# Layer 0 attention from two score products instead of product features, with TensorE's instructions in program order

## The chip, the cores and the metric

The kernel runs on one core of a Trainium2 chip. The time is what the device takes for one execution, in microseconds (us). It is the median of 11 executions, and one more execution was taken with the hardware profiler on. Engines are named as in the profile: PE (TensorE, matmuls), PEld (its weight loads), DVE (VectorE), ACT (ScalarE), POOL (GpSimd) and SP (the queue that issues most of the transfers). L457 is line 457 of the kernel.

## What is computed

Two layers run over x of 32 sequences x 256 positions x 128 channels, in f32. Each layer normalizes x, computes attention `s` and a mixture of experts `g`, and adds `s * silu(g)` to x. Only the attention of layer 0 changes its arithmetic. Cut to what matters, for 16 heads of 8 channels:

```python
q1, k1, q2, k2 = rotary(x @ Wq1.T), rotary(x @ Wk1.T), rotary(x @ Wq2.T), rotary(x @ Wk2.T)
v = x @ Wv.T
s1 = einsum('bqhd,bkhd->bhqk', q1, k1)
s2 = einsum('bqhd,bkhd->bhqk', q2, k2)
pattern = where(causal, s1 / 8 * (s2 / 8), 0)
y = einsum('bhqk,bkhd->bqhd', pattern, v) @ Wout.T
```

There is no softmax: the pattern is a plain product of two scores. Layer 0's experts (8 experts, two per row, GELU, hidden size 512) and a shared expert read the same normalized x. Layer 1 has its own attention and experts.

## The kernel before

The 8192 rows lie in 64 tiles of 128 rows (partitions) by 128 channels. Four tiles make a panel of 512 rows (two sequences); there are 16 panels. Layer 0 runs in five parts:

1. **Start.** `begin` (L286) normalizes a panel, turns it with four transposes (`pst`), and computes the gate's `logit`. Behind each panel after the first, two steps of attention are emitted.
2. **Route and dispatch.** `route0` (L303) finds each row's two experts and slots. `dispatch` then scatters the 64 tiles twice by indirect DMA on POOL's queue (L158), 128 scatters. `pace` holds them three at a time: a small POOL memset, `breath` (L142), waits for the last three. Three of four scatters are followed by a step of attention.
3. **Experts.** `experts` (L572) runs 72 blocks of 256 rows: weights `wt` by an indirect DMA on POOL, rows `xd` by a load on SP's queue that waits for all scatters, two transposes (`xdt`), four up projections 256 wide (`eup`, L592), four GELUs on ACT (L597), eight down projections (`edn`, L604) of the block before, and an add on DVE (`od`). A step of attention follows every eighth of its four yields per block.
4. **Combine.** `combine0` gathers a panel's rows back (`rows`, L623: eight indirect DMAs per panel, 128 in all, also three at a time), weighs them on DVE (L632), applies SiLU on ACT (L641), multiplies on POOL (`soin`, L642), adds to x on DVE (L643), normalizes and computes layer 1's `logit`. A list of due times sets which of its six parts follows which step of attention, a panel every six steps.
5. Layer 1, which begins with its own attention at about 1256 us of the profile.

Attention is a generator, `attention0` (L514). It gives a step for each of eight head pairs of a sequence, 16 steps a panel, and interleaves the preparation of the next sequence (`prepare`, L377), the shared expert (`shared`, L479), the sums over values and the output projection (`outward`, L498).

Before the change, the product s1 * s2 is written as one inner product: the 64 products of the 8 channels of q1 and q2 make a feature vector, likewise k1 and k2. `prepare` projects (`psp`, L405), multiplies by cosines and sines on DVE (`tu`, L410), adds (`rot`, L418) and makes features (`feat`, L422: 1024 wide, on DVE, or on POOL beside the experts). `turn` (L440) transposes two heads' features at a time, four transposes, one ACT copy (L442). `pattern` then needs four matmuls over 64 rows (`pp`, L457) and one DVE instruction that multiplies by the causal mask (L459). Only the two diagonal blocks of 128 x 128 are computed so: the later half's queries see the first half through a `state` (`pss`, L429, masked on DVE at L432), and `values` adds the state's part (L469) and the diagonal blocks' part (L475) into `y`. So that four heads' values can be summed in place, `vz` holds each head's values in its own 8 of 32 columns, zero elsewhere.

PSUM has eight banks of 512 f32 columns: two for `turn`, two for `pp`, three for all other uses (`mm`), one for `y`. In layer 0 a scheduler sets the order of instructions on every engine, TensorE's too.

Lines that matter below, as they stand:

```python
nc.tensor.matmul(psp[:, w, c], lhsT=qk[r, 2 + c], rhs=qk[r, c], start=True, stop=True)   # L457
nc.vector.tensor_tensor(pat, psp, bc(bc(dmask, 1, 2), 1, 2), ALU.mult)                   # L459
nc.sync.dma_start(part[p], sos[p])                                                       # L511
nc.gpsimd.tensor_tensor(acc, acc, so[:, 0], ALU.mult)                                    # L642
```

Of the kernel before, what the change touches and what calls it, by code (L numbers as in the profile page):

```python
# [11 lines left out]
F32 = mybir.dt.float32  # L12
# [8 lines left out]
P = 128  # L21
# [35 lines left out]
def model_kernel(ctx: ExitStack, tc: tile.TileContext, a: dict, out: bass.AP):  # L57
# [163 lines left out]
    with ExitStack() as c0:  # L221
        w0 = c0.enter_context(tc.tile_pool(name="w0", bufs=1))
        wk = c0.enter_context(tc.tile_pool(name="wk0", bufs=2))
        ps_t = c0.enter_context(tc.tile_pool(name="ps_t", bufs=2, space=PSUM))
        ps_p = c0.enter_context(tc.tile_pool(name="ps_p", bufs=1, space=PSUM))
# [5 lines left out]
        cs = w0.tile([P, 2, 2, D], F32, name="cs")  # L231
# [6 lines left out]
        smask = w0.tile([P, NH // 2, 2, 32], F32, name="smask")  # L238
        dmask = w0.tile([P, P], F32, name="dmask")
# [15 lines left out]
        nc.scalar.dma_start(smask, a["smask"])  # L255
        nc.vector.tensor_scalar(dmask, tri, 1.0 / (D * D), None, ALU.mult)
# [28 lines left out]

        def begin(p, x):  # L286

            t = slice(p * TT, (p + 1) * TT)
            layernorm(wk, x, xn[:, t, :], TT)
            pst = mm_tile("pst")  # L290
# [4 lines left out]
            psg = mm_tile("psg")  # L295
# [4 lines left out]
            nc.vector.tensor_tensor(logit[:, t, :], pg, bc(gb, 1, TT), ALU.add)  # L300


        def route0():  # L303
            with ExitStack() as cr:
                rp = cr.enter_context(tc.tile_pool(name="rp0", bufs=1))
                (_, _, oh0), (_, _, oh1) = top2(rp, logit, NT)
                ohf, tot, pos = counted(rp, mm_tile, "g", oh0, oh1)

                psn = mm_tile("psn")
# [67 lines left out]
        def prepare(b, seq):  # L377
# [9 lines left out]
            xT = xTs[p]  # L387
            yield
            psv = mm_tile("psv")
            cols = [slice((b % 2) * S + c * P, (b % 2) * S + (c + 1) * P) for c in range(2)]  # L390
            for c in range(2):
                nc.tensor.matmul(psv[:, c * P : (c + 1) * P], lhsT=xT[:, cols[c]], rhs=wproj[:, 4, :],
                                 start=True, stop=True)
            v = wk.tile([P, P], F32, tag="v", name="v")
            nc.scalar.copy(v, psv[:, :P])
            pv = psv[:, : 2 * P].rearrange("p (i g j d) -> p i g j d", i=2, g=4, j=4)
            vz = vzs[b % 2]
            vv = vz.rearrange("p i (g j) (k d) -> p i g j k d", g=4, k=4)
            for j in range(4):
                nc.scalar.copy(vv[:, :, :, j, j, :], pv[:, :, :, j, :])  # L400
            seq.vz, seq.feat = vz, []
            yield
            for c in range(2):
# [5 lines left out]
                for u in range(2):  # L409
                    nc.vector.tensor_tensor(tu[:, u].rearrange("p (g d) -> p g d", d=D),  # L410
                                            psp.rearrange("p (g d) -> p g d", d=D),
                                            bc(cs[:, u, c, :], 1, 4 * NH), ALU.mult)
                yield
                r = wk.tile([P, 4, NH, D], F32, tag="rot", name="rot")
                rv = r.rearrange("p t h (u d) -> p (t h) u d", u=2)
                tv = tu.rearrange("p n (g u d) -> p n g u d", u=2, d=D // 2)
                for u in range(2):
                    nc.vector.tensor_tensor(rv[:, :, u, :], tv[:, 0, :, u, :], tv[:, 1, :, 1 - u, :],  # L418
                                            ALU.add)
                f = wk.tile([P, 2, NH * D * D], F32, tag="feat", name="feat", bufs=3)  # L420
                for n, eng in ((1, makers[1]), (0, makers[0])):
                    eng.tensor_tensor(f[:, n].rearrange("p (h i j) -> p h i j", i=D, j=D),  # L422
                                      bc(r[:, n], 3, D), bc(r[:, 2 + n], 2, D), ALU.mult)
                seq.feat.append(f)
                yield
            pss = mm_tile("pss").rearrange("p (m w c) -> p m w c", w=2, c=32)
            v4 = v.rearrange("p (w g c) -> p g w c", w=2, g=2)
            for m in range(NH // 2):
                nc.tensor.matmul(pss[:, m], lhsT=seq.feat[0][:, 1, m * P : (m + 1) * P],  # L429
                                 rhs=v4[:, m // 4], start=True, stop=True)  # L430
            seq.state = wk.tile([P, NH // 2, 2, 32], F32, tag="state", name="state")
            nc.vector.tensor_tensor(seq.state, pss, smask, ALU.mult)  # L432
            yield

        def turn(seq, m):

            pst = ps_t.tile([P, 512], F32, tag="t", name="ptr").rearrange("p (n c) -> p n c", n=4)
            for n in range(2):
                for c in range(2):
                    nc.tensor.transpose(pst[:, 2 * n + c], seq.feat[c][:, n, m * P : (m + 1) * P], ident)  # L440
            qk = wk.tile([P, 4, P], F32, tag="qk", name="qk", bufs=3)
            nc.scalar.copy(qk, pst)  # L442
            return qk


        pp = ps_p.tile([P, 2, 2, 2, P], F32, name="pp")
        turns = [0]

        def pattern(qk):

            pat = wk.tile([P, 2, 2, P], F32, tag="pat", name="pat", bufs=4)
            psp = pp[:, :, turns[0] % 2]
            turns[0] += 1
            for c in range(2):
                for w in range(2):
                    r = slice(64 * w, 64 * w + 64)
                    nc.tensor.matmul(psp[:, w, c], lhsT=qk[r, 2 + c], rhs=qk[r, c],  # L457
                                     start=True, stop=True)
            nc.vector.tensor_tensor(pat, psp, bc(bc(dmask, 1, 2), 1, 2), ALU.mult)  # L459
            return pat  # L460

        def values(y, seq, ms, done):

            first = ms[0] == 0
            last = ms[1] == NH // 2 - 1
            for w in range(2):
                for m in ms:
                    g = 2 * w + m // 4
                    nc.tensor.matmul(y[32 * g : 32 * g + 32, P:S], lhsT=seq.state[64 * w : 64 * w + 64, m, w],  # L469
                                     rhs=done[m][0][64 * w : 64 * w + 64, 1], start=first, stop=False)  # L470
            for c in range(2):
                for w in range(2):
                    for m in ms:
                        g = 2 * w + m // 4
                        nc.tensor.matmul(y[32 * g : 32 * g + 32, c * P : (c + 1) * P],  # L475
                                         lhsT=seq.vz[:, c, m + 8 * w, :], rhs=done[m][1][:, w, c],
                                         start=False, stop=last and c == 1)

        def shared(p, so):  # L479

            hs = wk.tile([P, NFC, PT], F32, tag="hs", name="hs")
# [6 lines left out]
            dn = mm_tile("dn").rearrange("p (i c) -> p i c", i=TT)  # L488
            for i in range(TT):
                for f in range(NFC):  # L490
                    nc.tensor.matmul(dn[:, i, :], lhsT=hs[:, f, i * P : (i + 1) * P],
                                     rhs=dnw[:, f, :], start=(f == 0), stop=(f == NFC - 1))
                if i < TT - 1:
                    yield
            nc.vector.scalar_tensor_tensor(so[:, 1], dn, 0.1, bc(dnb, 1, TT), ALU.mult, ALU.add)
            yield

        def outward(b, y):  # L498
# [11 lines left out]
            if b % 2:  # L510
                nc.sync.dma_start(part[p], sos[p])  # L511
            yield

        def attention0():  # L514


            order = (0, 4, 1, 5, 2, 6, 3, 7)
# [3 lines left out]
            ahead = turn(seqs[0], 0)  # L521
            owed = []
            tail = iter(())
            for b in range(B):
                seq = seqs[b]
                nxt = prepare(b + 1, seqs[b + 1]) if b + 1 < B else iter(())
                y = None
                done = {}
                for n, m in enumerate(order):
                    qk = ahead  # L530
                    if n < 7:
                        ahead = turn(seq, order[n + 1])
                    elif b + 1 < B:
                        for _ in nxt:
                            pass
                        ahead = turn(seqs[b + 1], 0)
                    done[m] = (qk, pattern(qk))
                    next(nxt, None)
                    if n % 2 == 0 and owed:
                        owed.pop()()  # L540
                    else:
                        next(tail, None)
                    if n % 2:
# [126 lines left out]
        def step():  # L670
# [6 lines left out]
            if n % 2:  # L677
                some(sh, 1)
# [519 lines left out]
```

## Time and profile before

| | us |
|---|---|
| median of 11 executions | 2210.42 |
| lowest, highest | 2204.13, 2217.14 |
| the profiled execution | 2209.47 |
| its span in the profile | 2207.7 |
| PE busy (share, instructions) | 1956.7 (89%, 18674) |
| DVE busy | 1234.3 (56%, 2609) |
| ACT busy | 968.4 (44%, 1977) |
| POOL busy | 659.1 (30%, 817) |
| mean granted clock of TensorE | 0.928 |

A group line of the profile names line, engine, operation, what it writes and reads, and a count; then busy time and mean nanoseconds of one, and the time its engine sat idle just ahead of it, with what ended that. Busy times of groups of one engine can overlap, since matmuls are pipelined. A wait line names who waited for whom, the sum, how often, and the longest. A shared column for "issue" is waiting that the profile can put down to nothing.

### The profile page before, as it was taken

The page shows a single profiled execution, that of the slowest core. Times are in us where ns is not written, and L with a number is a line of the kernel's source. Part 1 is how long each engine was busy: PE and PEld are TensorE (multiplying, and loading weights), DVE is VectorE, ACT ScalarE, POOL GpSimd, SP SyncE. Part 2 cuts the span into 40 slices and gives each one's busy share as a digit, 9 for nine tenths or more (in the row PEclk, how much of TensorE's full clock was granted, in tenths as well). Part 3 has the DMA queues.
Part 4 walks back from the last instruction along what each step waited for, and adds up shares of the span by engine and source line. Part 5 has one row for each costly group of instructions (what it writes and reads, how often), then busy time and mean ns, then how long its engine had stood idle before and what let it go on. Part 6 is the DMA issues. An engine that isn't in the chain of part 4 may idle for free.

```text
span 2207.7 us, 45584 instructions
## 1 busy us (share of the span) xinstructions
PE 1956.7 (89%) x18674; PEld 1441.7 (65%) x18674; DVE 1234.3 (56%) x2609; ACT 968.4 (44%) x1977; POOL 659.1 (30%) x817
## 2 busy tenths in 40 slices
PE   6999999699999998765969589999999995788898
PEld 4777677488888886544747466666677773556565
DVE  6666767432222224654768477777433335677776
ACT  5623333233334333434746346566311114565655
POOL 0005555413222222555530035544000004454300
PEclk9999999899999999877979789999999997788889
DMA  8702111135445443222220311110122212112100
GB/s 262 211 1 78 44 45 34 57 116 162 155 148 175 146 151 111 77 80 67 82 69 35 108 32 35 36 35 27 49 72 72 72 55 56 52 54 60 44 26 11
DMA packets 131456, 176.80 MB, mean 80 GB/s; under 512 B 16304, under 2 KB 94659, under 8 KB 131248
## 3 DMA queue, kind: packets, MB, share of 16 engines
q1 hardware_dynamic: 103056, 96.57, 13.6%
q0 software_dynamic: 26752, 76.03, 11.5%
q8 instruction: 148, 2.42, 0.5%
q10 hardware_dynamic: 1440, 1.27, 0.2%
q14 instruction: 60, 0.49, 0.1%
HBM read 104.78 MB, written 69.21 MB: 79 GB/s over the span
## 4 chain that ended last, share of the span: by engine, by line
PE 42%; DMA 4%; POOL 3%; ACT 3%; issue 2%; DVE 1%; POOLq 0%; ACTq 0%; DVEq 0%; SPq 0%
PE apsT L853 6%; PE apav L862 6%; PE mpsd L1027 5%; PE mpsu L1014 5%; PE apsc L838 3%; PE apsc L831 2%; DMA rows<-moe,gidx 2%; PE pp L457 2%; DMA rows<-moe,slot 1%; POOL rows L623 1%; PE apsf L873 1%; PE apsv L815 1%; POOL rows L1055 1%; PE ptr L440 1%; PE apsk L803 1%
## 5 line engine op out<-in xcount | busy, mean ns | idle before, releaser
L457 PE MATMUL pp<-qk 64*128 64x128 f32 x2048 | 210.0, 309 | 106.4 <-DVE pat L459 54.4
L442 ACT COPY qk<-ptr 128x512 f32<-128x512 f32 x256 | 149.2, 586 | 352.9 <-PE y L469 270.9
L457 PEld LDWEIGHTS pp<-qk 64*128 64x128 f32 x2048 | 148.2, 192 | 177.7 <-issue 128.3
L459 DVE TENSOR_TENSOR pat<-pp,dmask 128x512 f32<-128x512 f32 x256 | 175.6, 686 | 128.6 <-PE pp L457 127.6
L855 ACT COPY apT<-apsT 124x512 f32<-124x512 f32 x256 | 146.8, 585 | 212.1 <-PE apsT L853 211.2
L1055 POOL DMA_INDIRECT rows<-moe,gidx x128 | 122.7, 959 | 333.6 <-ACT aqT L800 281.9
L862 PEld LDWEIGHTS apav<-ava,apT 124*64 124x64 f32 x4096 | 143.2, 140 | 113.2 <-issue 53.6
L158 POOL DMA_INDIRECT disp<-xn,slot x128 | 135.3, 1057 | 220.4 <-DVE state L432 171.0
L846 DVE TENSOR_REDUCE amx<-apsc 128x4 f32<-128x496 f32 x256 | 160.1, 667 | 72.3 <-PE apsc L838 72.0
L853 PE MATMUL apsT<-ident,apr 128*124 128x128 f32 x1024 | 169.2, 299 | 29.2 <-ACT apT L855 14.6
L608 DVE TENSOR_TENSOR od<-edn,wt 128x256 f32<-128x256 f32 x72 | 30.6, 425 | 286.1 <-PE edn L604 286.1
L862 PE MATMUL apav<-ava,apT 124*64 124x9 f32 x4096 | 166.6, 207 | 22.7 <-ACT apT L855 21.6
L597 ACT ACTIVATE ha<-eup,wt 128x256 f32<-128x256 f32 x288 | 119.2, 471 | 128.3 <-PE eup L592 125.4
L440 PE MATMUL ptr<-ident,feat 128*128 128x128 f32 x1024 | 170.0, 284 | 0.6 <-DVE feat L422 0.3
L848 ACT ACTIVATE apr<-apr 128x496 f32<-128x496 f32 x256 | 149.6, 618 | 30.2 <-DVE apr L847 30.1
L847 DVE TENSOR_TENSOR apr<-apsc,amx 128x496 f32<-128x496 f32 x256 | 159.5, 665 | 0.0
L563 POOL DMA_INDIRECT wt<-in_wexp,wrow x72 | 69.0, 959 | 296.4 <-DVE xdT L585 263.6
L623 POOL DMA_INDIRECT rows<-moe,slot x128 | 131.7, 1029 | 65.6 <-issue 29.0
L853 PEld LDWEIGHTS apsT<-ident,apr 128*124 128x124 f32 x1024 | 119.3, 149 | 47.4 <-ACT apT L855 19.7
L158 POOL DMA_INDIRECT disp<-xn,sidx x128 | 125.9, 984 | 80.7 <-DVE sidx L958 27.3
L440 PEld LDWEIGHTS ptr<-ident,feat 128*128 128x128 f32 x1024 | 119.6, 145 | 43.1 <-issue 38.0
L604 PEld LDWEIGHTS edn<-wt,ha 128*128 128x128 f32 x1152 | 137.7, 192 | 8.6 <-ACT ha L597 4.7
(217 smaller groups left out, 3673.0 us busy)
## 6 DMA issues: line engine op xcount, KB each, us to landing
disp<-zero SPq DMA_DIRECT2D x17, 1024.0 KB, 6.9
xd<-disp SPq DMA_DIRECT2D x72, 128.0 KB, 2.0
moe<-od SPq DMA_DIRECT2D x72, 128.0 KB, 2.0
x<-in_x SPq DMA_DIRECT2D x32, 256.0 KB, 3.1
part<-so SPq DMA_DIRECT2D x16, 512.0 KB, 3.0
soin<-part SPq DMA_DIRECT2D x16, 512.0 KB, 3.7
xd<-disp SPq DMA_DIRECT2D x32, 256.0 KB, 2.6
moe<-od SPq DMA_DIRECT2D x32, 256.0 KB, 2.0
```

The source lines that it names most:

```text
L158: ins = pace(lambda: nc.gpsimd.indirect_dma_start(out=self.dst[:, :], out_offset=bass.IndirectOffsetOnAxis(ap=idx, axis=0), in_=rows, in_o ...
L440: nc.tensor.transpose(pst[:, 2 * n + c], seq.feat[c][:, n, m * P : (m + 1) * P], ident)
L442: nc.scalar.copy(qk, pst)
L457: nc.tensor.matmul(psp[:, w, c], lhsT=qk[r, 2 + c], rhs=qk[r, c], start=True, stop=True)
L459: nc.vector.tensor_tensor(pat, psp, bc(bc(dmask, 1, 2), 1, 2), ALU.mult)
L623: pace(lambda: nc.gpsimd.indirect_dma_start(out=rows[:, k, i, :], out_offset=None, in_=moe0[:, :], in_offset=bass.IndirectOffsetOnAxis(ap= ...
L846: nc.vector.tensor_reduce(mx, sv, AX.X, ALU.max)
L847: nc.vector.tensor_tensor(to, sv, bc(mx, 2, NK), ALU.subtract)
L848: nc.scalar.activation(to, to, AF.Exp)
L853: nc.tensor.transpose(psT[:NK, j, :], pr[:, 4 * g + j, :], ident)
L855: nc.scalar.copy(pT[:NK], psT[:NK])
L862: nc.tensor.matmul(avv[u * QB : (u + 1) * QB, h, :], lhsT=pT[:NK, j, u * QB : (u + 1) * QB], rhs=va[:NK, 2 * st + u, h, :], start=True, st ...
```

## The change

It computes s1 and s2 themselves. `prepare` multiplies by cosines and sines on ACT, one column of every four per instruction, and transposes the four rotated tensors whole, four transposes per 128 rows; ACT writes the keys, and the queries four times, each time scaled by a mask (`qmask`) that leaves one of every four heads and has the 1/8. So 32 partitions hold four heads, and a matmul of 32 rows of keys against the four masked copies side by side (4 x 128 columns) gives four heads' scores in one bank. `score` does four of these, one per group of 32 rows, into four banks.

The work of a sequence is now three units (key block, query block) = (0,0), (0,1), (1,1), with two half-units each: `score` of s1 and `keep` (on the diagonal, DVE multiplies by the causal mask; off it, ACT copies), then `score` of s2 and `weigh` (DVE multiplies the two). Values of a unit are 16 matmuls, due after the next unit's first score. There is no state and no feature.

```diff
+        ps_s = c0.enter_context(tc.tile_pool(name="ps_s", bufs=4, space=PSUM))
...
+                for u in range(2):
+                    for i in range(D // 2):
+                        nc.scalar.activation(tu[:, u, i :: D // 2], psp[:, i :: D // 2], AF.Copy,
+                                             scale=cs[:, u, c, i : i + 1])
...
+            def turn(c):
+                ptr = mm_tile("ptr").rearrange("p (t n) -> p t n", t=4)
+                for t in range(4):
+                    nc.tensor.transpose(ptr[:, t], r[c][:, t], ident)
+                at = slice(c * P, (c + 1) * P)
+                nc.scalar.copy(seq.k[:, :, at], ptr[:, 2:4])
+                for j in range(4):
+                    nc.scalar.activation(seq.q[:, :, j, at], ptr[:, 0:2], AF.Copy,
+                                         scale=qmask[:, j : j + 1])
...
+        def score(seq, n, kc, qc):
+            banks = [s_tile("s").rearrange("p (j q) -> p j q", j=4) for _ in range(4)]
+            for g in range(4):
+                r = slice(32 * g, 32 * g + 32)
+                nc.tensor.matmul(banks[g], lhsT=seq.k[r, n, kc * P : (kc + 1) * P],
+                                 rhs=seq.q[r, n, :, qc * P : (qc + 1) * P], start=True, stop=True)
+            return banks
+        def keep(banks, diag):
+            s1 = wk.tile([P, 4, 4, P], F32, tag="s1", name="s1")
+            for g in range(4):
+                if diag:
+                    nc.vector.tensor_tensor(s1[:, g], banks[g], bc(tri, 1, 4), ALU.mult)
+                else:
+                    nc.scalar.copy(s1[:, g], banks[g])
+            return s1
+        def weigh(s1, banks):
+            pat = wk.tile([P, 4, 4, P], F32, tag="pat", name="pat", bufs=3)
+            for g in range(4):
+                nc.vector.tensor_tensor(pat[:, g], banks[g], s1[:, g], ALU.mult)
             return pat
+        def values(y, seq, pat, n, kc, qc):
+            for j in range(4):
+                for g in range(4):
+                    nc.tensor.matmul(y[32 * g : 32 * g + 32, qc * P : (qc + 1) * P],
+                                     lhsT=seq.vz[:, kc, 4 * g + j, :], rhs=pat[:, g, j],
+                                     start=(n == 0 and j == 0), stop=(n == 2 and j == 3))
...
-                nc.sync.dma_start(part[p], sos[p])
+                nc.scalar.dma_start(part[p], sos[p])
...
+                slots = iter((("n",), ("n",), ("s",), ("n",), ("n", "s"), ("n", "o", "s")) if b % 2 == 0
+                             else (("n",), ("n", "s"), ("s",), ("n",), ("n", "s"), ("n", "o")))
+                kinds = {"n": nxt, "s": sh}
+                for n, (kc, qc) in enumerate(units):
+                    diag = kc == qc
+                    s1 = keep(score(seq, 0, kc, qc), diag)
+                    pay(1)
+                    for k in next(slots):
+                        next(tail if k == "o" else kinds[k], None)
                     yield
+                    owed.append((seq, weigh(s1, score(seq, 1, kc, qc)), n, b))
+                    for k in next(slots):
+                        next(tail if k == "o" else kinds[k], None)
+                    yield
...
+            turned(0)
...
+                    yield
+                    if i + 1 < NB:
+                        turned(i + 1)
...
+        SPP = 12
...
+        in_order = {mybir.EngineType.PE}
+        with tc.manual_schedule(engines=in_order):
...
+            for n, _ in enumerate(dispatch()):
+                if n % 8 in (0, 2, 3, 5, 6):
+                    step()
...
+            for n, _ in enumerate(experts()):
+                if n % 4 == 1:
+                    step()
```

The rest of it: PSUM's banks become four for `s`, three for `mm`, one for `y`, and the gate's, the route's and the experts' tiles now take theirs from `s`. A panel has 12 steps, not 16: two per panel from the fourth on in the start (27 in all), five per eight scatters (80), one per two expert blocks (36; an expert block has two yields now, not four), and the other 49 in the loop of the combines, whose list of due times is unchanged. `begin` becomes a generator of three parts, run one panel behind another. In `experts` the rows of the next block are transposed (`turned`) ahead of the down projections of the block before. TensorE's instructions of layer 0 stand in program order; the scheduler still orders the other engines. The slot letters mean the next sequence's preparation (`n`), the shared expert (`s`) and the output (`o`). Buffers shrink: `hs` has one, not two, `xd` three, not four; `dn` is summed in two halves. The `part` store moves from SP's queue to ACT's.

More of the change, by code (lines that the diff above doesn't have):

```diff
@@ L387, in prepare, with rotate @@
             xT = xTs[p]
+            cols = [slice((b % 2) * S + c * P, (b % 2) * S + (c + 1) * P) for c in range(2)]
             yield
[L389 to L403, printed above, removed]
+            seq.q = wk.tile([P, 2, 4, S], F32, tag="q", name="q")
+            seq.k = wk.tile([P, 2, S], F32, tag="k", name="k")
+            seq.vz = vzs[b % 2]
+            r = {}
+            def rotate(c):
                 psp = mm_tile("psp")
@@ L424, in prepare @@
[L424 to L432, printed above, removed]
@@ L433, in prepare @@
-            yield
[L435 to L453, printed above, removed]
-            for c in range(2):
[L455 to L459, printed above, removed]
-            return pat
@@ L462, in values @@
[L462 to L477, printed above, removed]
+                    for i in range(D // 2):
+                        nc.scalar.activation(tu[:, u, i :: D // 2], psp[:, i :: D // 2], AF.Copy,
+                                             scale=cs[:, u, c, i : i + 1])
```

255 lines of the change are left out of this document (119 added, 136 removed).

## The prediction

> **What bounds the kernel now.** I read the busy time by stretches first, cut where layer 0 changes its work: start and gate up to 175 us, scattering of rows to 420, a short stop, the expert blocks to 853, the gathers to 1131, the rest of layer 0 to 1256. The columns are the stretch, its length, then busy time and instruction count of PE, PEld, DVE, ACT and POOL, the granted clock, the DMA share and GB/s.
> ```profile
> core 0: us, PE busy (x) PEld busy (x) DVE busy (x) ACT busy (x) POOL busy (x), PEclk, DMA share, GB/s
> 175.00:420.00 245.00, 245.00 (x2648) 172.88 (x2646) 163.41 (x240) 86.56 (x196) 135.97 (x164) 1.00 0.16 50
> 420.00:451.00 31.00, 13.94 (x120) 9.72 (x120) 9.70 (x16) 2.52 (x5) 7.45 (x9) 0.67 0.20 68
> 451.00:853.00 402.00, 401.12 (x2989) 334.40 (x2989) 100.91 (x223) 154.14 (x370) 96.10 (x85) 1.00 0.48 152
> 853.00:1131.00 278.00, 193.52 (x1868) 138.50 (x1865) 161.45 (x398) 124.95 (x249) 148.15 (x181) 0.83 0.25 78
> 1131.00:1256.00 125.00, 107.15 (x1152) 79.50 (x1150) 84.85 (x215) 73.12 (x150) 9.57 (x13) 0.93 0.13 43
> ```
> TensorE is never idle while rows are scattered and while experts run, and nearly always after the last gather (to 1225 us); it is the bound there. During the gathers it has 84 us of idle. The 128 scatters go out from 175.6 to 431.5 us, 2.0 us each, three at a time, so a floor of 256 us stands beside the first stretch; the 128 gathers go out from 853.8 to 1130.8 us. From 1256 us on (951 us) the change touches nothing.
>
> The costliest groups of the page say what fills TensorE and its neighbours in attention.
> ```profile
> L457 PE MATMUL pp<-qk 64*128 64x128 f32 x2048 | 210.0, 309 | 106.4 <-DVE pat L459 54.4
> L442 ACT COPY qk<-ptr 128x512 f32<-128x512 f32 x256 | 149.2, 586 | 352.9 <-PE y L469 270.9
> L459 DVE TENSOR_TENSOR pat<-pp,dmask 128x512 f32<-128x512 f32 x256 | 175.6, 686 | 128.6 <-PE pp L457 127.6
> L440 PE MATMUL ptr<-ident,feat 128*128 128x128 f32 x1024 | 170.0, 284 | 0.6 <-DVE feat L422 0.3
> ```
> A matmul on f32 has two records, a transpose one. In 200 to 420 us there are 79 `pat` instructions, 8 to a sequence: 220/(79/8) = **22.3 us a sequence** at a full TensorE. Counting `pp` records (64 a sequence), the expert stretch holds 4.6 sequences, so its 72 blocks take (402 - 4.6 x 22.3)/72 = 4.16 us each.
>
> The waits of 853 to 1131 us, and ACT's groups of 415 to 452 us, show the two stops.
> ```profile
> PEld pp L457 <- issue: 89.9, 33, 22.8
> DVE x L643 <- POOL soin L642: 82.9, 8, 24.7
> POOL breath L142 <- DMA rows<-moe,slot: 75.2, 41, 4.9
> PE pp L457 <- DVE pat L459: 51.1, 6, 19.9
> ```
> ```profile
> L508 ACT COPY so<-pso 128x256 f32<-128x256 f32 x1 | 0.4, 373 | 20.4 <-DMA part<-so 20.4
> ```
> VectorE, in order, stands behind POOL's multiply, which stands among the gathers, and attention stops with it. At 419 us ScalarE waited 20.4 us for a `part` transfer, which sat on SP's queue behind the `xd` loads that wait for the last scatter.
>
> **The change on TensorE.** In the rows of 200 to 420 us, a sequence's present matmuls sum to 27.5 us of busy time (32 pp x 0.179, 32 ptr x 0.157, 32 values x 0.080, 16 state x 0.106, 8 pss x 0.25, and 10.4 for psp, psv, psu, dn, pso and pxt, which stay). They share 22.3 us, a factor 0.81. Out go pp, state, pss and 24 of 32 transposes. In come 16 more values, 1.3 us, and 6 scores of four 32-row matmuls. Their nearest rows are in layer 1's trace, with the durations of VectorE and ScalarE on a 512-wide bank (start, duration, then the group):
> ```profile
> 1343.48 1.09 PE L838 MATMUL apsc<-akb,aqT 32*64 32x496 f32 x16
> ...
> 1345.80 1.25 DVE L847 TENSOR_TENSOR apr<-apsc,amx 128x496 f32<-128x496 f32 x2
> ```
> ```profile
> 38.27 1.06 ACT L442 COPY qk<-ptr 128x512 f32<-128x512 f32 x2
> ```
> Eight matmuls over four row groups and two column halves took 1.09 us, as long as one; one full 512-wide `psp` took 1.07. So a score costs 1.09, bounded by 4 x 1.07 = 4.3 us if the groups came one after another. The new sum is 22.1, x 0.81 = **17.9 us**, 4.4 less. That saving can be had only if the evictions keep up.
>
> **Evictions.** Now TensorE hands VectorE one bank per head pair; then it hands over 24 banks a sequence. Two f32 instructions on a bank took 1.25 us, starts 0.6 apart, so four end 2.46 us after the first began; ScalarE's copies of four end after 2.03 (1.06 for two). VectorE: 20 banks x 0.60 + 4 rot x 0.38 + 0.35 = 13.9 us, against 15.3 before (8 x 0.69 pat, 4 x 0.65 tu, 4 x 0.40 rot, 4 x 1.22 feat, 0.69 state). ScalarE goes from about 8 to about 13 us: 16 scaled 128-wide copies, 8 of 256, 4 bank copies. The scaled copy of every fourth column (`tu`) is not in the trace: a plain 128-wide copy took 0.265 us, the scaled 128-wide `soin` 0.32 apart (4 in 1.29), `xn` 0.49. I take 0.30, nearest `soin`; ends 0.17 (apart, from four `vz` in 0.57) and 0.49.
>
> **The pace of a half-unit.** A score fills all four `s` banks, so the next score waits for each bank. I walked the twelve half-units of two sequences with these rules: a matmul starts when TensorE arrives and its bank is free (0.15 after the eviction); it ends 1.09 later; evictions run in order, 0.60 apart; TensorE does its slot's work (1.0 to 3.4 us: values 1.1, psp or psu 0.95, eight dn 1.85, psv or pso 0.45, a turn 0.6) before the next score. In the order built, ScalarE has eight `tu` (2.4 us) ahead of the third half-unit's copies, and VectorE's rot waits for eight more ahead of the fifth's last bank. From the first score, one sequence's half-units end at 3.9, 6.4, 10.5, 13.2, 18.2 and 20.7 us; the two take 21.25 and 20.55, **3.5 us a half-unit**, 21 a sequence. So of the 4.4 us that TensorE saves, 3.1 turn into waits for banks: the pace gains 1.3.
>
> *A rule against the change:* the Trainium skill, TensorEngine Tiling (Array Packing), section PSUM Bottleneck, says that tiling speeds up the matmuls but not the evacuation. The rows agree: 1.09 us to fill, 2.46 to empty. By the rule alone (evictions end to end, 24 banks) a sequence would be near 14 us, so it is not the whole bound. The skill's page TensorE: Matmul & The Clock Gate, in its table of measured speedups, gives 3.07 times for four row groups; no run here shows it for 128 output columns. By it, a score would be an estimated 1.4 us and a half-unit 3.8.
>
> **Stage by stage, for a half-unit h.** The 192 steps are dealt anew: 27 in the start, 80 beside the scatters, 36 beside the experts, 49 after (before, in sequences of 8: 30, 96, 36 and 94).
> - Start: the first score comes near 32 us. Each half-unit there also carries 0.75 us of gate work (L292 and L298: 11.6 + 18.4 us over 16 panels, x 0.81, two half-units each), and the gate's transposes take a bank of the same ring, 0.5 more (ScalarE's copy out of it takes 0.58). 32 + 27 x (3.5 + 1.25) = 160 us, against the last `logit` at 141 us. TensorE, now in fixed order, then holds all attention behind the route's counts for some 17 us (they came 19 us after the last logit before), and 80 x 3.5 = 280 us bring it to 457. The scatters give 160 + 34 + 256 + 9 = 459 (34 and 9 as before). Against 451: **+8**. The 20.4 us wait goes, since `part` leaves SP's queue for ScalarE's; the scatters' end is late next, so it is worth nothing by itself. `part` costs ScalarE 16 issues of 0.32 to 0.45 us, seen at its first ones.
> - Experts: blocks 72 x 4.16 = 299. Each of the 36 half-units follows an up projection whose two banks must be drained by four GELUs (ending 2.9 us after its start, TensorE done at 1.8 to 2.0), some 0.6 net. 36 x 4.1 = 148. Sum 447 against 402: **+45**. The shorter prefetch of `xd` (3 buffers) I cost at nothing: its loads land in 2.0 us; if its cover went, 72 x up to 2.
> - Gathers and rest: 49 half-units are 8.2 sequences, against 11.65. Before, 7.25 were done while the gathers ran, the rest after. Floor: 278 as now, 2.6 for the last landing, 19.5 for a panel's chain (its `soin` load went out at 1236.7, layer 0 ended at 1256) = 300. If VectorE is stopped as often as now, 7.25 sequences again take 278 and the last 0.95 x 21 + 31 (that chain and the other panels' turns) make 329. I take 315 against 403: **-88**.
> Sum -35. Since 27 + 80 + 36 half-units lie on this path, it moves by 143 us for each us of h: 143 h - 537. The profiled execution took 2209.5 us (span 2207.7), 0.9 below the median of 11, so 2209.5 - 35 = **2175 us**.
>
> **Rivals.** (a) *Faster, 2128:* waits for banks overlap slot work better, h = 3.0, TensorE-bound (17.9/6). The scatters' floor counts, 32 + 27 x 4.25 + 34 + 256 + 9 = 446, -5; experts 299 + 36 x 3.6, +27; the rest at its floor, -103: -81. For it: VectorE has only 13.9 us of work. Against: six full drains of the ring a sequence. (b) *Slower, 2260:* ScalarE's scaled copies set the pace. If `tu` costs 0.49 (as `xn`), each group of eight takes 3.9 instead of 2.4 us, twice a sequence ahead of a bank: h = 4.0, 143 x 4.0 - 537 = +35; the start, where ScalarE already has some 9.6 us of work in the 9.5 us of a panel (4.5 of attention, 5 of layernorm and table loads of 1.28), adds 5.3 copies x 0.19 on 13.5 panels, 14: +49. It decides from h = 3.76. For it: strided PSUM reads are unseen. Against: `soin`'s 0.32. (c) *The groups don't run side by side:* h rises by up to 3.2 us, +450; L838 speaks against it. A lower clock belongs to (b): the stretches with gaps had 0.83 against 1.00 in full ones.
>
> **The numbers.** Forecast (h 3.3 to 3.75) 0.42, (a) 0.20, (b) 0.34, (c) 0.04. A measurement here tells about 0.2%, 4.4 us. Faster: 0.57, same 0.06 (around h = 3.76), slower 0.37. Range: 2105 ((a) without the experts' 0.6 a half-unit, -22) to 2290 ((b) with the rest at 329, +14, and most of a doubled 0.6, +22); (c) is left out.
>
> **What would show it.** Steps right: a score's records end within 1.2 us; TensorE's idle in the scatter stretch is named `pat`, `s1` or `s`; first expert matmul near 459; expert stretch near 447; `rows` gathers end near 1185, layer 0 near 1220. Wrong: half-units over 3.8 us there, `tu` above 0.4 us, or the gathers spreading past 280 us because VectorE waits for POOL as before.

## The result and the profile after

The changed kernel takes **2380.47 us** (median of 8 runs, 2378.73 to 2383.53), the kernel before 2210.69 (31 runs): a ratio of **1.0772, 95% interval 1.0761 to 1.0784**. The forecast was 2175, faster. The profiled execution has a span of 2374.9 us, 167 more than before. The first four experiments below ran on the chip of this result, one timed execution each, and the other eight on two further chips on which the kernel before takes 2284 and 2285 us (layer 1, which the change does not touch, took 950 to 956 us on the first chip and 1016 to 1038 on those), so for these eight the whole time is given as a ratio to the kernel before on the same chip, and layer 0 by the stretches of one profiled execution.

Busy time by stretches, changed kernel, cut at the same events as in the prediction (start, scatters, the attention left over after them, experts, gathers, the rest of layer 0); the columns are the prediction's:
```profile
0.00:181.00 181.00, 150.74 (x980) 89.68 (x980) 90.93 (x293) 111.02 (x288) 4.02 (x19) 0.88 0.51 143
...
208.00:460.00 252.00, 251.53 (x2182) 134.73 (x2182) 170.86 (x301) 145.34 (x415) 129.21 (x172) 0.99 0.17 54
460.00:493.00 33.00, 32.37 (x302) 17.95 (x302) 21.62 (x39) 20.86 (x59) 0.96 (x1) 1.00 0.10 34
493.00:1013.00 520.00, 436.52 (x2994) 332.82 (x2993) 145.33 (x294) 194.12 (x501) 64.67 (x69) 0.96 0.37 118
1013.00:1291.00 278.00, 197.18 (x963) 98.46 (x962) 133.97 (x391) 137.16 (x316) 141.16 (x181) 0.64 0.26 79
1291.00:1425.00 134.00, 110.24 (x776) 69.50 (x776) 67.45 (x178) 66.12 (x147) 7.66 (x12) 0.76 0.10 35
```
The expert stretch grew from 402 to 520 us, and in it TensorE, never idle before, now stands for 84 us. The gathers still take 278 us, but with the clock at 0.64 instead of 0.83, and 134 us of work remain after them, although this kernel has less attention left there: 144 `s` records, 18 half-units or 3 sequences, against 4.4 sequences before.

| stretch of layer 0, us | before | forecast | after |
|---|---|---|---|
| until the first expert matmul | 451 | 459 | 492.7 |
| from there to the first gather | 403 | 447 | 522 |
| from there to the end of layer 0 | 402 | 315 | 410 |

The groups of the page that answer to `pp`, `pat` and the expert block's:
```profile
L445 PE MATMUL s<-q,k 32*128 32x512 f32 x1536 | 423.9, 716 | 71.7 <-DVE pat L463 59.2
L463 DVE TENSOR_TENSOR pat<-s,s 128x512 f32<-128x512 f32 x384 | 241.9, 683 | 170.6 <-PE s L445 170.4
...
L595 PE MATMUL eup<-xdT,wt 128*128 128x256 f32 x576 | 153.0, 413 | 84.1 <-DMA wt<-in_wexp,wrow 83.0
```
The last line was not among the prediction's suspects: the up projection waits 83.0 us for the experts' weights. The two kernels issue the same expert instructions, and before the change that wait was 0.8 us:
```profile
L592 PE MATMUL eup<-xdT,wt 128*128 128x256 f32 x576 | 142.2, 389 | 0.8 <-DMA wt<-in_wexp,wrow 0.8
```

The attention itself behaves as forecast. A piece of the timeline beside the scatters (start, duration, group):
```profile
385.31 1.14 PE L445 MATMUL s<-q,k 32*128 32x512 f32 x8
...
386.47 2.48 DVE L463 TENSOR_TENSOR pat<-s,s 128x512 f32<-128x512 f32 x4 [1.23 <-PE s L445]
...
388.27 1.86 PE L445 MATMUL s<-q,k 32*128 32x512 f32 x8
...
394.19 2.29 ACT L406 ACTIVATE tu<-psp,cs 128x128 f32<-128x128 f32 x8 [1.84 <-PE psp L400]
```
The first score (eight records) finds its four banks free and ends in 1.14 us: the row groups run side by side. Four evictions take 2.48 us, and a score that gets its banks one by one takes 1.86. Eight scaled copies take 2.29. Counting `s` records (eight a half-unit), 208 to 488 us hold 630, close to 79 half-units: 3.6 us each, near the forecast's h of 3.5.

### The profile page after: what moved, and what is told of

Read it like the earlier page. It is cut to its first block, busy times and chain, and to the rows that moved or that the text cites. A ratio compares the mean times of both kernels' runs of the same rounds, so it can differ in the third digit from the quotient of the medians.

```text
span 2374.9 us, 42400 instructions
## 1 busy us (share of the span) xinstructions
PE 2040.3 (86%) x16882; PEld 1347.1 (57%) x16882; DVE 1251.3 (53%) x2737; ACT 1121.3 (47%) x2547; POOL 605.8 (26%) x801
## 5 line engine op out<-in xcount | busy, mean ns | idle before, releaser
L445 PE MATMUL s<-q,k 32*128 32x512 f32 x1536 | 423.9, 716 | 71.7 <-DVE pat L463 59.2
L463 DVE TENSOR_TENSOR pat<-s,s 128x512 f32<-128x512 f32 x384 | 241.9, 683 | 170.6 <-PE s L445 170.4
L445 PEld LDWEIGHTS s<-q,k 32*128 32x128 f32 x1536 | 151.3, 204 | 251.0 <-DVE pat L463 141.3
L595 PE MATMUL eup<-xdT,wt 128*128 128x256 f32 x576 | 153.0, 413 | 84.1 <-DMA wt<-in_wexp,wrow 83.0
L454 DVE TENSOR_TENSOR s<-s,tri 128x512 f32<-128x512 f32 x256 | 162.9, 683 | 76.1 <-PE s L445 75.6
L406 ACT ACTIVATE tu<-psp,cs 128x128 f32<-128x128 f32 x512 | 147.5, 512 | 97.6 <-PE psp L400 70.7
L158 POOL DMA_INDIRECT disp<-xn,slot x128 | 123.1, 962 | 253.0 <-DVE pat L463 203.9
L595 PEld LDWEIGHTS eup<-xdT,wt 128*128 128x128 f32 x576 | 112.1, 205 | 104.2 <-issue 88.6
L628 POOL DMA_INDIRECT rows<-moe,slot x128 | 124.1, 969 | 69.1 <-issue 30.1
L609 PE MATMUL edn<-wt,ha 128*128 128x128 f32 x1152 | 140.3, 275 | 0.0
```

The source lines that it names most:

```text
L158: ins = pace(lambda: nc.gpsimd.indirect_dma_start(out=self.dst[:, :], out_offset=bass.IndirectOffsetOnAxis(ap=idx, axis=0), in_=rows, in_o ...
L406: nc.scalar.activation(tu[:, u, i :: D // 2], psp[:, i :: D // 2], AF.Copy, scale=cs[:, u, c, i : i + 1])
L445: nc.tensor.matmul(banks[g], lhsT=seq.k[r, n, kc * P : (kc + 1) * P], rhs=seq.q[r, n, :, qc * P : (qc + 1) * P], start=True, stop=True)
L454: nc.vector.tensor_tensor(s1[:, g], banks[g], bc(tri, 1, 4), ALU.mult)
L463: nc.vector.tensor_tensor(pat[:, g], banks[g], s1[:, g], ALU.mult)
L595: nc.tensor.matmul(pu, lhsT=wt[:, f * P : (f + 1) * P], rhs=xdT, start=True, stop=True)
```

## The experiments

**Experts: the weights' buffer (`wt4`).** Where the 83 us arise is seen in the timeline of the changed kernel, in a pair of blocks of which the first has a half-unit and the second none:
```profile
639.17 0.94 POOL L558 DMA_INDIRECT wt<-in_wexp,wrow  x1 [2.80 <-DVE od L613]
...
640.19 3.60 PE L595 MATMUL eup<-xdT,wt 128*128 128x256 f32 x8 [2.25 <-DMA wt<-in_wexp,wrow]
...
649.33 0.42 DVE L613 TENSOR_TENSOR od<-edn,wt 128x256 f32<-128x256 f32 x1 [1.36 <-PE edn L609]
...
650.52 0.94 POOL L558 DMA_INDIRECT wt<-in_wexp,wrow  x1 [10.42 <-ACT tu L406]
...
651.08 1.95 PE L609 MATMUL edn<-wt,ha 128*128 128x128 f32 x16
...
655.14 1.10 PE L595 MATMUL eup<-xdT,wt 128*128 128x256 f32 x4 [2.11 <-DMA wt<-in_wexp,wrow]
```
Read it backwards: the up projection of 655.14 stood 2.11 us for weights whose fetch was issued at 650.52, 4.6 us earlier. With three buffers a fetch can go out only when the block three before it has read its weights for the last time (`od`, which ended at 649.75; the line names `tu`, but the fetches that name `od`, at 639.17 and 654.26, also go out some 0.8 us after its end). What TensorE then still has before the new block, here the down projection of 651.08, must cover issue and landing: a block without a half-unit takes some 3.9 us in all. Before, the planner strewed small pieces of attention over nearly all blocks: from one fetch to the next it was 4.8 us or more in 64 of 68 cases (3.8 to 7.9). Now a whole half-unit goes to every second block, and from fetch to fetch it is 3.6 or 3.7 us in 34 of 68 cases and 9.1 to 13.1 in the others: the short blocks have no cover.
```diff
-            wt = ek.tile([P, NW], F32, tag="wt", name="wt", bufs=3)
+            wt = ek.tile([P, NW], F32, tag="wt", name="wt", bufs=4)
-                    ha = ek.tile([P, NFC, TB], F32, tag="ha", name="ha", bufs=3)
+                    ha = ek.tile([P, NFC, TB], F32, tag="ha", name="ha", bufs=2)
```


> The changed kernel with four buffers for an expert block's weights instead of three, paid for by two instead of three for the GELU's output (which is freed before the next one needs it). Theory (the weight fetch of 4 to 4.5 us has only 3.9 us of cover in the block pairs without a half-unit, because its buffer comes free so late): the expert stretch falls from 520 to 435-455 us, the 83 us of waits of the up projection for the weights go under 15, and the whole time falls to about 2300. Rival (the half-unit's full ring of banks and the GELUs' drains cost it): the stretch stays within 10 us of 520, the whole within 10 of 2380, and the waits move from the weights to the banks. In both the gathers and the rest of layer 0 stay at 411 us.

Measured: 2269.48 us against 2211.03 of the kernel before beside it. Its expert stretch, and what its up projection waits for in the whole run:
```profile
492.00:904.00 412.00, 411.07 (x2989) 321.70 (x2992) 145.41 (x295) 193.85 (x501) 63.74 (x68) 1.00 0.47 147
```
```profile
its engine sat idle before it (us, times) until:
  DVE xdT L579: 1.1, 2
```
The waits for weights are gone, TensorE is full again, and the stretch is 412 us, below the theory's 435. The gathers and the rest kept 407. The rival falls. The stretch gained more than its 83 us of waits: 72 blocks at the prediction's 4.16 leave 112 us for 36 half-units, 3.1 each, so by this sum no net GELU drain is left to see, and the forecast's 4.1 was too much.

**The order of TensorE (`noord`).** The three `manual_schedule` blocks of layer 0 were taken out.
```diff
-        with tc.manual_schedule(engines=in_order):
+        with ExitStack():
```


> The changed kernel without the fixed order of TensorE in layer 0: the planner orders it, as it ordered the kernel before. Rival (the fixed order is what costs the time): whole time 2230 or less, with gains in all stretches. Theory (fixed order costs only where it puts a whole half-unit at every second block; the products and their evictions are as many): the expert stretch falls from 520 to 450-490, the gathers and the rest stay within 25 us of 411 since VectorE still stands behind the gathers, whole 2320-2360.

Measured: 2368.89 us; first expert matmul at 491.7, experts 511 us, gathers and rest 411. The rival falls: the fixed order is not what costs. The theory's number for the experts (450 to 490) missed too: given the same program, the planner does not spread the half-units (34 of 68 gaps between fetches are still 3.7 to 4.1 us), and the experts gain only 11 us.

**Gathers: who stops VectorE (`mult`, `dvem`).** The waits of the changed kernel from 1013 to 1291 us (total, times, longest):
```profile
POOL breath L142 <- DMA rows<-moe,slot: 81.2, 40, 5.3
DVE soin L637 <- DMA rows<-moe,slot: 75.3, 52, 5.2
PEld s L445 <- DVE pat L463: 75.0, 40, 9.7
DVE x L648 <- POOL soin L647: 51.8, 8, 13.1
```
In the kernel before, from 853 to 1131 us, VectorE's wait for gathered rows was
```profile
DVE soin L632 <- DMA rows<-moe,slot: 16.3, 10, 4.2
```
One of the stops of the changed kernel, in order of time:
```profile
1138.92 0.94 POOL L628 DMA_INDIRECT rows<-moe,slot  x1 [0.30 <-issue]
...
1141.50 0.10 POOL L142 MEMSET breath<- 128x1 f32 x1 [1.63 <-DMA rows<-moe,slot]
1141.64 1.26 POOL L647 TENSOR_TENSOR soin<-soin 128x512 f32<-128x512 f32 x1
1142.93 0.69 DVE L648 TENSOR_TENSOR x<-x,soin 128x512 f32<-128x512 f32 x1 [8.08 <-POOL soin L647]
...
1144.06 0.68 DVE L463 TENSOR_TENSOR pat<-s,s 128x512 f32<-128x512 f32 x1
...
1144.79 4.45 PE L445 MATMUL s<-q,k 32*128 32x512 f32 x8 [6.50 <-DVE pat L463]
```
POOL's multiply waits its turn among gathers, which go three at a time; VectorE's addition waits 8.08 us for the multiply; the evictions of a score stand behind the addition in VectorE's queue; the next score, all four of whose banks are full, waits 6.50 us. Then it gets its banks one by one, behind the evictions, at half clock, and takes 4.45 us. Two edits, the first alone in `mult`, both in `dvem`:
```diff
-            nc.gpsimd.tensor_tensor(acc, acc, so[:, 0], ALU.mult)
+            nc.vector.tensor_tensor(acc, acc, so[:, 0], ALU.mult)
...
         now = t0
-        with tc.manual_schedule(engines=in_order):
+        with tc.manual_schedule(engines=in_order | {mybir.EngineType.DVE}):
```


> The changed kernel with the combine's multiply moved from POOL, where it stands among the gathers, to VectorE. Theory (VectorE is stopped by things that follow the pace of the gathers: 52 us behind POOL's multiply, 75 us behind the gathered rows themselves): the 52 us of waits go, 16 x 0.6 = 10 us of VectorE work come, gathers and rest fall from 411 to 370-390 us, whole about 2350. Rival 1 (POOL's place is the whole cause): 411 falls to 330 or less. Rival 2 (the rows' waits simply grow to the same end): 411 stays within 10.

Measured: 2320.67 us; from the first gather to the last `logit` 352 us, 57 less. More than the theory's 20 to 40, and still short of the 330 of rival 1; VectorE's waits for gathered rows rose from 75 to 89 us, so they are a second stop, as the theory has it:
```profile
DVE soin L637 <- DMA rows<-moe,slot: 89.3, 57, 5.2
```

> As mult (the multiply on VectorE), and in the gathers' stretch VectorE too keeps the written order, in which a panel's weighing stands six half-units behind its gathers, instead of the planner's order. Theory (what stretches a half-unit there from 3.5 to 9.2 us is that VectorE's queue has weighings that wait for gathers between the four evictions of a half-unit): the waits for gathered rows go from 75 us to under 25, some 43 or more of the 49 half-units are done while the gathers run, the clock rises from 0.64 to over 0.8, gathers and rest fall from 411 to 310-335 us, whole about 2295. Rival (half-units are slow there of themselves, at the low clock, or for ScalarE): under 36 half-units, 411 falls by less than 30.

Measured: 2301.79 us; from the first gather to the end of layer 0 332 us (after: 410). VectorE's waits for these rows are down to 3.9 us. All the half-units now end before the gathers do:
```profile
1011.00:1241.00 230.00, 216.60 (x1586) 113.09 (x1584) 158.39 (x365) 145.47 (x353) 86.56 (x118) 0.88 0.25 76
1241.00:1344.00 103.00, 34.66 (x152) 24.96 (x148) 63.87 (x218) 58.12 (x110) 40.49 (x53) 0.52 0.29 87
```
The last `pat` is at 1241.1. In the first line the 49 half-units take 4.7 us each, where the changed kernel took 9.2 (30 of them in 278 us), and the clock is 0.88. Over the gathers as a whole it was 0.78, short of the 0.8 expected. What stood in VectorE's queue was the cause, and not the half-units themselves; why they still take 4.7 us here and not 3.6 was not taken apart. The second line is new: the gathers (now to 1328.6 us) had been held by weighings due late, and 103 us of little but combines follow.

**The start (`tuve`).** Until the routing, the rotation's products go back to VectorE, two instructions a bank.
```diff
+                    if early[0]:
+                        nc.vector.tensor_tensor(tu[:, u].rearrange("p (g d) -> p g d", d=D),
+                                                psp.rearrange("p (g d) -> p g d", d=D),
+                                                bc(cs[:, u, c, :], 1, 4 * NH), ALU.mult)
+                    else:
...
-                for u, op in enumerate((ALU.add, ALU.subtract)):
+                for u, op in enumerate((ALU.add, ALU.add if early[0] else ALU.subtract)):
```


> The changed kernel with the rotation's products back on VectorE (two instructions a bank, as before) until the routing is done, and on ScalarE (eight scaled copies) after it. Theory (in the first 90 us ScalarE is full: 26 of each 30 us, half-units of 6.6 us against 4.8 in the 90 us after): the last gate logit comes at 165-173 us instead of 181, the first expert matmul at 477-485 instead of 493, the whole falls by 8-15 us to about 2368. Rival (the low clock of 0.72 or the loads of that stretch set its pace, not ScalarE): both stay within 4 us.

Measured: a ratio of 1.085 (1.0716 to 1.0984; two executions) on a chip where the change itself was not timed, so the whole tells nothing. The last gate logit came at 168.7 us, as the theory had it (without the edit it came at 181 to 185 on the other two chips): ScalarE's load did set the start's pace, for 12 of the 21 us that it was late. Between 30 and 90 us ScalarE's busy time fell from 52 to 46 us, and the clock rose from 0.72 to 0.83. But the first expert matmul came at 499.4 instead of 477 to 485.

**One part of the change alone (`b_part`).** The kernel before, with the store of a panel on ScalarE's queue.
```diff
-                nc.sync.dma_start(part[p], sos[p])
+                nc.scalar.dma_start(part[p], sos[p])
```


> One part of the change alone: the kernel before, with the store of a finished panel issued on ScalarE's queue instead of SP's. Theory (at 419 us ScalarE waited 20.4 us for that store, behind expert loads that wait for the last scatter, and TensorE was busy for 14 of the next 31 us): TensorE fills that stretch with attention that need not be done later, 5-15 us faster, 2196-2206. Rival (that attention is off the path, as the forecast held when it costed it at nothing): within 4 us of 2211.

Measured: a ratio of 0.9981 (0.994 to 1.0022), an interval that includes what both the theory and the rival expect. The profile leans to the theory, though the kernel before was profiled on another chip: first expert matmul at 443.0 us instead of 451.3, end of layer 0 at 1243 instead of 1256, and the 20.4 us wait is not there.

**The same stop in the kernel before (`b_mult`).** Its edit is that of `mult`.

> The kernel before, with the combine's multiply moved from POOL to VectorE as in mult. Theory (both kernels lose time in the gathers because VectorE stands behind what follows the gathers' pace): 89 us of VectorE's waits for POOL go, the 403 us of gathers and rest fall by 25-60, the whole to 2150-2186. Rival (in the kernel before that stop was covered, its TensorE having other work): less than 10 us.

Measured: a ratio of **0.9753 (0.9638 to 0.9868; two executions)**; from the first gather to the end of layer 0 344 us instead of 402, the rest of layer 0 unmoved. That stop was not covered there either. VectorE's waits for gathered rows are 21 us here, against 89 in `mult` with the same edit.

**The fixes together (`best1`, `wt4dvem`, `every4`, `every4t`).** The first has `wt4`, `dvem` and `tuve`.

> The changed kernel with wt4, dvem and tuve together (four weight buffers, multiply on VectorE, VectorE in written order while the gathers run, the rotation on VectorE until the routing). Theory (three separate losses, in stretches that follow one another): the gains add, 2380 - 111 - 79 - 10 = 2180, between 2168 and 2195, faster than the kernel before. Rival (what is gained in one stretch is lost in the next): 2211 or more.

Measured: a ratio of 0.9998 (0.9952 to 1.0043), level with the kernel before, where the theory asked for 0.98 to 0.99. The rival's number (2211 or more) lies within that interval, but not for its reason: experts 415 us, gathers and rest 334, so there the gains add. What is missing lies before them: last `logit` at 166.0, but first expert matmul at 504.2.

> The changed kernel with wt4 and dvem together, the rotation left on ScalarE. Theory (two losses in stretches that follow one another): the gains add, 0.99 of the kernel before (2380 - 111 - 79 = 2190 against 2211), layer 0 ending near 1237 us. Rival (best1's product came out level with the kernel before because the two gains overlap): layer 0 ends at 1253 or later, as in best1.

Measured: 1.0056 (1.0025 to 1.0086); layer 0 ends at 1265 us, later than `best1`. The theory's 1237 missed; the rival's number (1253 or later) came, but its reason did not: experts 415, gathers and rest 331, so the gains do not overlap; what is off is the first expert matmul, at 519.4, though up to that point this kernel is the same as `wt4`, which had it at 492.4 on the first chip. The two stretches side by side, `wt4` first:
```profile
300.00:460.00 160.00, 160.00 (x1400) 85.82 (x1403) 108.82 (x190) 92.79 (x266) 81.03 (x108) 1.00 0.15 48
```
```profile
300.00:460.00 160.00, 156.63 (x1278) 81.16 (x1277) 97.96 (x172) 87.04 (x245) 81.30 (x110) 0.93 0.15 48
```
The granted clock was 1.00 on the one chip and 0.93 on the other, and TensorE got through 368 `s` records there and 327 here: 3.5 and 3.9 us a half-unit. The kernel before kept 0.99 to 1.00 beside its scatters, in its own form on the first chip and in its edited forms on the others (`b_part`, `b_mult_part`).

`every4` adds to `wt4dvem` combines that are due sooner; `every4t` adds `tuve` to that.
```diff
-        EVERY, LATER = 6, (0, 6, 7, 8, 11, 13)
+        EVERY, LATER = 4, (0, 6, 7, 8, 11, 13)
```


> wt4dvem with a panel's combine due every four half-units instead of six. In dvem the 49 half-units were done 230 us after the experts, 4.7 each, and then the combines had 103 us to themselves at a clock of 0.52, while POOL's gathers had waited 52 us for weighings. Theory (the gathers, 278 us by themselves, are the floor once nothing holds them): 335 falls to 305-318 us, layer 0 ends 17-30 us before wt4dvem's. Rival (more combine work among the half-units stops VectorE again): within 8 us of wt4dvem, or later.

Measured: 0.9933 (0.9897 to 0.9968). From the first gather on 319 us instead of 331; layer 0 ends at 1247, 18 us before `wt4dvem`'s, of which 5 come from an earlier first expert matmul. The gathers take 284 us, 6 above their floor. That is the theory at the edge of its range (it asked for 318 or less); the 35 us after them are the last panels' combines.

> every4 with the rotation on VectorE until the routing, as in tuve. In tuve and best1 the last gate logit came 13-15 us earlier, but the half-units beside the scatters took 3.9 us instead of 3.5, and the first expert matmul came no earlier. If that was the chip of those runs (its clock was granted at 0.90 to 0.95 in that stretch), layer 0 ends 10-15 us before every4's. If it belongs to the kernel (the planner's order of VectorE and ScalarE in that stretch): at the same time or later.

Measured: 0.9875 (0.9828 to 0.9922), an interval that overlaps `every4`'s; layer 0 ends at 1248, no sooner. The last `logit` is 12 us earlier (168.6), the first expert matmul 4 (510.1), and the granted clock in the first 105 us of scatters is 0.87, against 0.92 in `every4`. So in the profiles the start's gain is given back, at a lower clock, which by the test set down ahead speaks for the kernel and not for the chip. That is not settled: the profiled execution was the slowest of the four (2280 us against a median of 2262), `every4`'s was not (2266 against 2272), and the first chip was not tried.

> The kernel before with two small edits and no new products: the combine's multiply on VectorE and the panel's store on ScalarE's queue. Theory (both edits took time out of layer 0 in separate stretches, 57 and 13 us by the profiles of b_mult and b_part): layer 0 ends near 1186 us, 0.968 of the kernel before, and sooner than the best of the changed kernels here, because a product saves TensorE 4.4 us a sequence but gives most of it back to bank drains. Rival (the new products are worth more once their stops are taken away): every4 is the faster of the two.

Measured: **0.9692 (0.9633 to 0.9751)**, the fastest of all: layer 0 ends at 1195 us, against the theory's 1186. Against `every4` on the same chip it has its first expert matmul 66 us sooner (448 and 514), experts 10 us shorter, and the rest 23 us longer. The rival falls: with the stops of both taken away, the new attention is ahead on this chip only in the last stretch.

## Why the prediction was wrong, step by step

The miss is 202 us of span (2374.9 against a forecast of 2172.7): 34 before the experts, 75 in them, 95 after them, less some 1.5 in layer 1.

- **The pace of a half-unit, 3.5 us: right** (3.6 beside the scatters), and so were its terms: a score 1.14 for 1.09, four evictions 2.48 on VectorE for 2.46 and 2.1 on ScalarE for 2.03, `tu` 0.26 apart for 0.30. Rival (c) is out. The table that the prediction took from the Trainium skill (TensorE: Matmul & The Clock Gate, section Measured speedup vs the span model) gave 3.07 times for four row groups; here one full 512-wide `psu` took 1.02 and the four groups of a score 1.14, some 3.6 times. The measurement decides.
- **Start, +8: it was +42.** The step that failed is 3.5 + 1.25 for each half-unit of the start. From 30 to 90 us there were 9 half-units, 6.7 us each, with ScalarE busy for 52 of 60 us and the clock at 0.72 to 0.73; from 90 to 181 us there were 18, 5.1 us each, near the forecast's 4.75. `tuve` showed ScalarE to be 12 of the 21 us; what the other 9 are stays open. The forecast had this cost, 14 us, but only in rival (b), tied to a slow `tu`; the row that ScalarE "already has some 9.6 us of work in the 9.5 us of a panel" stood in the text, and was charged to nothing in the forecast itself. The route's stretch, which by the forecast holds attention for 17 us, took 27 with only ten `s` records in it: ten more. The rest before the experts is near the forecast's 80 x 3.5 = 280 us: the other 630 records took 280 us, and 5 us of other work follow.
- **Experts, +45: it was +120.** The failed step is what it left out. The text priced the `xd` prefetch (rightly at nothing: 1.1 us of waits) and the GELU drains, and did not look at POOL's weight fetch, though the change moved attention past it: from small pieces in all blocks to a whole half-unit in every second. `wt4` shows 108 us to be due to this. What was priced was too dear: half-units 3.1 and not 4.1 us in `wt4`, where TensorE is full.
- **Gathers and rest, -88: it was +8.** The failed step is "if VectorE is stopped as often as now, 7.25 sequences again take 278", which made 329 the worst case. The stop was seen, and its cause (VectorE behind POOL's multiply), but not that the new kernel is more open to it. Before, VectorE stood only 16.3 us for gathered rows, and now 75.3; 5 sequences were done, not 7.25. `mult` took away 57 us, `dvem` 77, and `every4` came to 319: near the forecast's 315. A likely reason, read from the code and not tested by itself: a half-unit fills all four banks, so the next score stands behind four evictions in the queues of VectorE or ScalarE, where before one bank of a head pair was enough.
- **`part` on ScalarE's queue, nothing: not refuted.** In the kernel before the ratio was 0.9981, with 1 inside its interval.
- **Rivals.** The slower one (b) had the sign, by another mechanism: h stayed near 3.5 on this chip. None of the three had the two stretches that made the result, and so the range missed it.

With the weights' cover and VectorE's order mended, about half of the forecast's gain of 35 us would be there on the first chip, by an estimate from two separate runs (2376.7 - 108 - 77 = 2192 against 2209.5); on the others the mended kernel measured 0.9998 and 1.0056. The new products are a weak lever: by the prediction's sums, whose pace held, TensorE saves 4.4 us a sequence, and 3.1 of them go to bank drains. Two one-line edits to the kernel before brought more.

## What to carry to other kernels

When a change moves one stream of work into larger pieces, list every prefetch that the small pieces had covered, and compare for each the shortest block now with issue plus landing: an average that grew says nothing. Before counting on an engine that is half idle, read what stands in its queue ahead of the work: an in-order VectorE that also serves gathers passes on their pace. Look for such a stop in the kernel as it is first; here taking it away was worth more than the new algorithm.

## What the runs showed of the hardware

- **The clock follows the stops.** Where the score waited up to 9.7 us (1013 to 1291 us), the granted clock was 0.64; the sixteen values matmuls of a unit took 1.94 us there (at 1111.44 us) and 1.08 at the full clock. In `dvem`, the same half-units at 0.88 took 4.7 instead of 9.2 us. The Trainium skill, TensorE: Matmul & The Clock Gate, section HAM oscillation — how this bites in real kernels, asks for no idle gaps of TensorE above some 3.4 us; these rows agree with it.
- **Other chips, other clocks.** The same instructions beside the scatters ran at 0.96 before and 1.00 after 300 us on one chip, and at 0.92 and 0.93 on another, where in the latter 160 us no wait was longer than 2.6 us; the granted clock there was not evenly lower but either full or half (0.50 from 348 to 354 us, 1.00 from 355 to 402), half for some 24 of the 160 us. The rule just quoted does not cover these spans, and why they come without long stops was not settled.
- **Scaled copies of every fourth column from PSUM** on ScalarE go out 0.26 us apart (eight in 2.29), sooner than the 0.32 of the scaled 128-wide `soin` before; the four unscaled `vz`, at 0.17, were closer still.
